# Softmax without maxima, and attention matmuls of several heads on separate row and column groups of the TensorE array

## Chip, cores and metric

The kernel runs on one core of one Trainium2 chip. A time is the device time of the run in microseconds (us). All runs quoted repeat within 0.3% except where the text says so. TensorE multiplies, VectorE and ScalarE read the results, GpSimd does little (busy for 2% of the kernel before). "Clock" is the share of its full clock that TensorE was granted.

## The reference

Sixteen batch elements of 256 channels and 32 x 32 = 1024 tokens, all in float32. Layer a is a softmax attention with 4 heads of 64 channels. Layer b is a group norm, a softmax attention with 8 heads of 32 channels, a second group norm and an MLP of width 1024. Cut to what matters:

```python
# layer a: x [16, 256, 32, 32], 4 heads of 64
qkv = (xs @ w_proj + b_proj).reshape(B, S, 4, 192)          # xs: tokens x channels
attn = softmax(einsum('bihd,bjhd->bijh', q, k) * 64 ** -0.5, axis=2)
res = einsum('bijh,bjhd->bihd', attn, v).reshape(B, S, 256) @ w_out + b_out + xs
# layer b: 8 heads of 32
q, k, v = split(group_norm(x) @ qkv_w.T)
attn = softmax(einsum('bhnd,bhmd->bhnm', q, k) * 32 ** -0.5 + phys_bias)   # phys_bias: per head
x = x + einsum('bhnm,bhmd->bhnd', attn, v) @ proj_w.T + proj_b
x = x + mlp_w2 @ gelu(mlp_w1 @ group_norm(x) + mlp_b1) + mlp_b2
```

## The kernel before

One element after the other; per element: q, k, v of layer a, its attention, projection and group norm, the same for layer b, then the MLP. Attention takes an item (512 queries of one head) at a time, in three products. First come the scores with queries on the partitions, only to find each query's maximum (`s`). Then the scores again with keys on the partitions (`w`), with the negated maximum brought in by an extra row, 33 rows instead of 32. Last comes the weighted sum (`acc`), whose ones columns give the denominator. One head at a time is on the array: 32 or 64 of its 128 rows in `s` and `w`, and in layer b 64 of its 128 columns in `acc`.

```python
        def maxima(i, j):                       # product s, 128 queries x 1024 keys
            s = ps_s.tile([P, S], F32, tag="s", ...)
            for u in range(NT):
                nc.tensor.matmul(s[:, u * TB : (u + 1) * TB],
                    qA[lo : lo + D, sl, qb * P : (qb + 1) * P],
                    kA[lo : lo + D, sl, u * TB : (u + 1) * TB], start=True, stop=True)
            nc.vector.tensor_reduce(negmax[i][:, j : j + 1], s, AX.X, ALU.max, negate=True)

        def weights(i, j):                      # product w, 256 keys x 512 queries
            for u in range(2):
                kb = 2 * j + u
                nc.tensor.matmul(s[:, u, :],
                    kA[lo : lo + D + 1, sl, kb * P : (kb + 1) * P],
                    qA[lo : lo + D + 1, sl, t * TB : (t + 1) * TB], start=True, stop=True)
            nc.scalar.activation(e, s, AF.Exp, scale=scale, bias=...)
            pending.append((i, j, e))

        def weigh():                            # product acc: v and ones columns
            for u in range(2):
                nc.tensor.matmul(acc[: 2 * D, :], vA[:, kb, h].rearrange("p o d -> p (o d)"),
                    e[:, u, :], start=(kb == 0), stop=(kb == SB - 1))
        # ... transposes that place the maxima cut
        for i, (t, h) in enumerate(items):
            place_maxima(i)
            for j in range(steps):
                if i + 1 < len(items) and j < QT:
                    maxima(i + 1, j)
                if pending:
                    weigh()
                weights(i, j)
```

Of the kernel before, what the change touches and what calls it, by code (L numbers as in the profile page):

```python
# [8 lines left out]
F32 = mybir.dt.float32  # L9
AF = mybir.ActivationFunctionType  # L10
ALU = mybir.AluOpType
AX = mybir.AxisListType

P = 128
# [3 lines left out]
HEADS1, D1 = 8, 32  # L18


@with_exitstack
def kernel(
    ctx: ExitStack,
    tc: tile.TileContext,
    x: bass.AP,        # [B, C, S]
    w_proj: bass.AP,   # [C, HEADS0 * 3 * D0], columns ordered (head, q|k|v, d)
    b_proj: bass.AP,
    w_out: bass.AP,    # [C, C]
    b_out: bass.AP,
    gn1_w: bass.AP,  # L30
    gn1_b: bass.AP,
    gn2_w: bass.AP,
    gn2_b: bass.AP,
    qkv_wT: bass.AP,   # [C, 3 * C]
    proj_wT: bass.AP,  # [C, C]
    proj_b: bass.AP,
    phys_bias: bass.AP,
    mlp_w1T: bass.AP,  # [C, HID]
    mlp_b1: bass.AP,
    mlp_w2T: bass.AP,  # [HID, C]  # L40
    mlp_b2: bass.AP,
    out: bass.AP,      # [B, C, S]
):
    nc = tc.nc
    B, C, S = x.shape
    HID = mlp_w1T.shape[1]
    CC = C // P            # channel chunks
    SB = S // P            # 128-token blocks
    TB = 512               # tokens per wide matmul
    NT = S // TB  # L50
    HC = HID // P
    QT = TB // P           # 128-token blocks in a wide one
    GSZ = C // GROUPS      # channels per group

    const = ctx.enter_context(tc.tile_pool(name="const", bufs=1))
    act = ctx.enter_context(tc.tile_pool(name="act", bufs=1))
    work = ctx.enter_context(tc.tile_pool(name="work", bufs=3))
    small = ctx.enter_context(tc.tile_pool(name="small", bufs=4))
    ps_s = ctx.enter_context(tc.tile_pool(name="ps_s", bufs=2, space=bass.MemoryType.PSUM))
    ps_m = ctx.enter_context(tc.tile_pool(name="ps_m", bufs=4, space=bass.MemoryType.PSUM))  # L60

    def load_x(b):
        t = act.tile([P, CC, S], F32, tag="x", name=f"x_{b}", bufs=2)
        for cc in range(CC):
            nc.sync.dma_start(t[:, cc, :], x[b, cc * P : (cc + 1) * P, :])
        return t

# [1 line left out]
    wp = const.tile([P, CC, 3, HEADS0, D0], F32, name="wp")  # L69
    for cc in range(CC):  # L70
        for t in range(3):
            nc.scalar.dma_start(
                wp[:, cc, t],
                w_proj[cc * P : (cc + 1) * P, :].rearrange(
                    "p (h t d) -> p t h d", t=3, d=D0
                )[:, t],
            )
    xs = {0: load_x(0)}

    # q and k biases with two heads on the partitions, v's along the free axis  # L80
    bp = b_proj.rearrange("(g i t d) -> i t d g", i=2, t=3, d=D0)
    bqk = const.tile([P, 2, HEADS0 // 2], F32, name="bqk")
    for i in range(2):
        for t in range(2):
            nc.gpsimd.dma_start(bqk[i * D0 : (i + 1) * D0, t, :], bp[i, t])
    bv = const.tile([P, HEADS0, D0], F32, name="bv")
    nc.gpsimd.dma_start(
        bv,
        b_proj.rearrange("(h t d) -> t h d", t=3, d=D0)[2].partition_broadcast(P),
    )  # L90
    pb = const.tile([P, HEADS1], F32, name="pb")
    nc.gpsimd.dma_start(pb, phys_bias.partition_broadcast(P))

    pbs = const.tile([P, HEADS1], F32, name="pbs")
    nc.vector.tensor_scalar(pbs, pb, float(D1) ** 0.5, None, ALU.mult)
# [5 lines left out]

    bo = load_vec(b_out, CC, "bo")
    g1w = load_vec(gn1_w, CC, "g1w")
    g1b = load_vec(gn1_b, CC, "g1b")
    g2w = load_vec(gn2_w, CC, "g2w")
    g2b = load_vec(gn2_b, CC, "g2b")
    pjb = load_vec(proj_b, CC, "pjb")
    m1b = load_vec(mlp_b1, HC, "m1b")
    m2b = load_vec(mlp_b2, CC, "m2b")

    def load_mat(w, name):
        k, n = w.shape
        t = const.tile([P, k // P, n], F32, name=name)
        nc.scalar.dma_start(t, w.rearrange("(c p) n -> p c n", p=P))
        return t

    wo = load_mat(w_out, "wo")
    wq = load_mat(qkv_wT, "wq")
    wpj = load_mat(proj_wT, "wpj")
    w1 = load_mat(mlp_w1T, "w1")  # L120
    w2 = load_mat(mlp_w2T, "w2")

    ident = const.tile([P, P], F32, name="ident")
    make_identity(nc, ident)
    # gavg[p, m] = 1 / GSZ where channels p and m share a group, else 0
    gind = const.tile([P, P // GSZ], F32, name="gind")
    nc.vector.tensor_reduce(
        gind, ident.rearrange("p (g j) -> p g j", j=GSZ), AX.X, ALU.add
# [9 lines left out]
    gavg = gavg.rearrange("p g j -> p (g j)")  # L138
    mhalf = const.tile([P, CC], F32, name="mhalf")
    nc.gpsimd.memset(mhalf, -0.5)  # L140
# [5 lines left out]
    # Head h lies in slot h // nb of qA and kA ([P, slots, S]), on the D partitions  # L146
    # from (h % nb) * 64 on. The partition after them holds ones in kA and, once
    # they are known, the queries' negated maxima in qA. vA ([P (key), SB, H, 2, D])
    # holds v and ones, so that the weighted sum comes with its denominator on D
    # further partitions.  # L150
    # Calls project(t, resT) when TB queries of all heads are in resT ([P, CC, S]).
# [102 lines left out]
    # y[:, co, t] = w^T src + bias + skip, tokens of t; bn_stats of y into stats  # L254
    def out_proj(key, w, nk, src, bias, skip, t, dst, stats):
        for co in range(CC):
            ps = mm_tile(f"{key}_{t}_{co}")
            for k in range(nk):
                nc.tensor.matmul(  # L259
                    ps,  # L260
                    w[:, k, co * P : (co + 1) * P],
                    src(k),
                    start=(k == 0),
                    stop=(k == nk - 1),
                )
            y = dst(co)
            nc.vector.scalar_tensor_tensor(  # L267
                y, ps, bias[:, co : co + 1], skip[:, co, t * TB : (t + 1) * TB],
                ALU.add, ALU.add,
            )  # L270
            if stats is not None:
                nc.vector.bn_stats(stats[:, co, t, :], y)

    def group_norm(key, src, stats, gw, gb):
        mv = small.tile([P, CC, 2], F32, tag="mv", name=f"mv_{key}")
        for cc in range(CC):
            nc.vector.bn_aggr(mv[:, cc, :], stats[:, cc].rearrange("p t k -> p (t k)"))
        ps = mm_tile(f"gm_{key}")
        mean_c = small.tile([P, CC], F32, tag="mean_c", name=f"mean_c_{key}")
        nc.vector.tensor_copy(mean_c, mv[:, :, 0])  # L280
        nc.tensor.matmul(ps[:, :CC], gavg, mean_c, start=True, stop=True)
        mean = small.tile([P, CC], F32, tag="mean", name=f"mean_{key}")
        nc.vector.tensor_copy(mean, ps[:, :CC])
        # variance of the group: mean over its channels of var_c + (mean_c - mean)^2
        dv = small.tile([P, CC], F32, tag="dv", name=f"dv_{key}")
        nc.vector.tensor_sub(dv, mean_c, mean)
        sq = small.tile([P, CC], F32, tag="sq", name=f"sq_{key}")
        nc.vector.tensor_mul(sq, dv, dv)
        tv = small.tile([P, CC], F32, tag="tv", name=f"tv_{key}")
        nc.vector.tensor_add(tv, sq, mv[:, :, 1])  # L290
        ps2 = mm_tile(f"gv_{key}")
        nc.tensor.matmul(ps2[:, :CC], gavg, tv, start=True, stop=True)
        ve = small.tile([P, CC], F32, tag="ve", name=f"ve_{key}")
        nc.vector.tensor_scalar(ve, ps2[:, :CC], EPS, None, ALU.add)
        rstd = small.tile([P, CC], F32, tag="rstd", name=f"rstd_{key}")
        nc.gpsimd.tensor_tensor(rstd, ve, mhalf, ALU.pow)
        a = small.tile([P, CC], F32, tag="ga", name=f"ga_{key}")
        nc.vector.tensor_mul(a, rstd, gw)
        ma = small.tile([P, CC], F32, tag="gma", name=f"gma_{key}")
        nc.vector.tensor_mul(ma, mean, a)  # L300
        c = small.tile([P, CC], F32, tag="gc", name=f"gc_{key}")
        nc.vector.tensor_sub(c, gb, ma)
        y = act.tile([P, CC, S], F32, tag="gn", name=f"gn_{key}")
        for t in range(NT):
            for cc in range(CC):
                sl = slice(t * TB, (t + 1) * TB)
                if cc % 2 == 0:
                    nc.vector.tensor_scalar(  # L308
                        y[:, cc, sl], src[:, cc, sl],
# [61 lines left out]
    for b in range(B):  # L371
        if b + 1 < B:
            xs[b + 1] = load_x(b + 1)
# [99 lines left out]
```

## Time and profile before

The three runs took 14661.59 to 14680.31 us, median 14663.05. Where they go, per batch element, from the starts of the phases in the trace (an attention counts from its first score product to the first product of the group norm after it, so with its projections; the two group norms, some 4 us each, are left out):

| phase | us per element before |
|---|---|
| layer a, attention and projection | 201.0 |
| layer b, attention and projection | 607.4 |
| layer b, q, k and v | 23.2 |
| MLP, from its first product to the next element's q, k, v | 57.2 |

The lines themselves are shown and read in the prediction below. A group line gives engine, operation, output and inputs, their sizes, the count, busy time, mean ns of one, and then the idle time before them with what ended it. A timeline line gives start, duration, engine and count of a run of like instructions. A windows line gives the stretch, then busy time and count of TensorE, its weight loads, VectorE, ScalarE and GpSimd, then the granted clock, the DMA share and GB/s.

### The profile page before, as it was taken

Reading aid. Unit: us, or ns where it says so; the run is one execution under the profiler, and the core shown is the slowest. Engines: PE = TensorE matmul, PEld = TensorE weight load, DVE = VectorE, ACT = ScalarE, POOL = GpSimd, SP = SyncE. Lnnn points to the kernel's source line nnn. Section 1 sums busy time; section 2 is a strip of 40 time slices with the busy share of each in tenths; the row PEclk is TensorE's granted clock in tenths of the full one; section 3 lists DMA queues with packets and bytes.
Section 4 is the critical chain, followed back from the end, with each engine's and each line's share of the span. In section 5 each row is a group of like instructions: output and inputs, shape, how many; then the busy total and the mean of one; then the engine's idle time right before and its main releaser. Section 6 shows DMA issues by size and latency. Waiting matters only on the chain.

```text
span 14689.8 us, 58040 instructions
## 1 busy us (share of the span) xinstructions
PE 14357.1 (98%) x24704; PEld 4764.6 (32%) x24704; DVE 4368.7 (30%) x4003; ACT 2188.0 (15%) x2336; POOL 258.7 (2%) x133
## 2 busy tenths in 40 slices
PE   9999999999999999999999999999999999999999
PEld 3233332333323333233332333323333233332333
DVE  3233232322323223232232322323223232232322
ACT  1111111111111111111111111111111111111111
POOL 0000000000000000000000000000000000000000
PEclk8686786867868668686686866868668686686866
DMA  0000000000000000000000000000000000000000
GB/s 21 0 3 3 3 3 0 3 3 3 3 0 3 3 2 4 0 3 3 2 4 0 3 3 2 5 0 3 3 3 3 0 3 3 3 0 0 3 0 3
DMA packets 19332, 41.62 MB, mean 3 GB/s; under 512 B 4704, under 2 KB 6240, under 8 KB 19072
## 3 DMA queue, kind: packets, MB, share of 16 engines
q1 hardware_dynamic: 13312, 33.56, 0.6%
q10 hardware_dynamic: 5296, 4.20, 0.1%
q8 instruction: 194, 3.18, 0.1%
q14 instruction: 66, 0.54, 0.0%
q0 software_dynamic: 464, 0.15, 0.0%
HBM read 21.12 MB, written 16.78 MB: 3 GB/s over the span
## 4 chain that ended last, share of the span: by engine, by line
PE 93%; issue 5%; DVE 2%; ACT 0%; POOL 0%; DMA 0%; ACTq 0%; POOLq 0%; DVEq 0%
PE acc_b L221 22%; PE s_b L169 19%; PE w_b L199 18%; PE s_a L169 7%; PE acc_a L221 7%; PE w_a L199 6%; PE m L420 3%; PE m L259 3%; PE qk_b L333 2%; PE qk_a L333 2%; PE row_b L184 1%; PE j L259 1%; PE v_a L356 1%; PE o L259 1%; PE v_b L356 1%
## 5 line engine op out<-in xcount | busy, mean ns | idle before, releaser
L221 PE MATMUL acc_b<-e_b,vA_b 128*64 128x512 f32 x4096 | 3566.7, 1025 | 6.0 <-ACT e_b L207 6.0
L169 PE MATMUL s_b<-kA_b,qA_b 32*128 32x512 f32 x4096 | 3060.5, 886 | 0.0
L199 PE MATMUL w_b<-qA_b,kA_b 33*128 33x512 f32 x4096 | 2864.9, 835 | 30.1 <-DVE qA_b L189 30.1
L176 DVE TENSOR_REDUCE nmax_b<-s_b 128x1 f32<-128x1024 f32 x1024 | 1253.7, 1224 | 4999.6 <-PE s_b L169 4995.4
L207 ACT ACTIVATE e_b<-w_b,pb 128x1024 f32<-128x1024 f32 x1024 | 1139.9, 1113 | 8376.4 <-PE w_b L199 8376.4
L199 PEld LDWEIGHTS w_b<-qA_b,kA_b 33*128 33x128 f32 x4096 | 945.8, 256 | 2288.7 <-issue 2269.2
L221 PEld LDWEIGHTS acc_b<-e_b,vA_b 128*64 128x64 f32 x4096 | 748.0, 211 | 2537.1 <-issue 2343.1
L169 PEld LDWEIGHTS s_b<-kA_b,qA_b 32*128 32x128 f32 x4096 | 916.1, 246 | 1667.9 <-issue 1451.9
L231 DVE RECIPROCAL rden_b<-acc_b 32x512 f32<-32x512 f32 x256 | 857.3, 3349 | 723.8 <-PE acc_b L221 723.8
L221 PE MATMUL acc_a<-e_a,vA_a 128*128 128x512 f32 x2048 | 1027.2, 627 | 11.8 <-ACT e_a L207 11.8
L169 PE MATMUL s_a<-kA_a,qA_a 64*128 64x512 f32 x2048 | 1028.7, 627 | 0.5 <-DVE nmax_a L176 0.5
L199 PE MATMUL w_a<-qA_a,kA_a 65*128 65x512 f32 x2048 | 984.1, 605 | 28.8 <-DVE qA_a L187 28.8
L176 DVE TENSOR_REDUCE nmax_a<-s_a 128x1 f32<-128x1024 f32 x512 | 626.0, 1223 | 1233.7 <-PE s_a L169 1232.1
L207 ACT ACTIVATE e_a<-w_a 128x1024 f32<-128x1024 f32 x512 | 523.9, 1023 | 2241.1 <-PE w_a L199 2236.1
L189 DVE TENSOR_SCALAR qA_b<-row_b,pbs 1x512 f32<-1x512 f32 x256 | 189.9, 742 | 1275.2 <-PE row_b L184 1274.2
L221 PEld LDWEIGHTS acc_a<-e_a,vA_a 128*128 128x128 f32 x2048 | 359.1, 193 | 639.5 <-issue 362.0
L199 PEld LDWEIGHTS w_a<-qA_a,kA_a 65*128 65x128 f32 x2048 | 394.4, 193 | 529.2 <-issue 506.2
L169 PEld LDWEIGHTS s_a<-kA_a,qA_a 64*128 64x128 f32 x2048 | 353.3, 190 | 577.4 <-issue 539.2
L420 PE MATMUL m<-gn_h,w 128*128 128x512 f32 x1024 | 480.3, 630 | 35.1 <-DVE gn_h L308 35.1
L231 DVE RECIPROCAL rden_a<-acc_a 64x512 f32<-64x512 f32 x128 | 430.0, 3359 | 253.4 <-PE acc_a L221 253.4
L259 PE MATMUL m<-g,w 128*128 128x512 f32 x1024 | 444.7, 592 | 0.0
L267 DVE SCALAR_TENSOR_TENSOR o<-m,m2b,x 128x512 f32<-128x512 f32 x64 | 48.1, 751 | 875.3 <-PE m L259 875.3
(98 smaller groups left out, 4119.8 us busy)
## 6 DMA issues: line engine op xcount, KB each, us to landing
x<-in_x_dram SPq DMA_DIRECT2D x32, 512.0 KB, 4.0
out_dram<-o SPq DMA_DIRECT2D x32, 512.0 KB, 2.8
w<-in_L_conv_mlp_w_dram ACTq DMA_DIRECT2D x2, 1024.0 KB, 9.3
wp<-in_L_conv_w_proj_dram ACTq DMA_DIRECT2D x6, 128.0 KB, 8.3
wq<-in_L_conv_qkv_w_dram ACTq DMA_DIRECT2D x1, 768.0 KB, 7.3
wo<-in_L_conv_w_out_dram ACTq DMA_DIRECT2D x1, 256.0 KB, 5.5
wpj<-in_L_conv_proj_w_dram ACTq DMA_DIRECT2D x1, 256.0 KB, 8.5
bv<-in_L_conv_b_proj_dram POOLq DMA_DIRECT2D x1, 128.0 KB, 8.2
```

Source lines behind the costliest of these rows:

```text
L169: nc.tensor.matmul(s[:, u * TB : (u + 1) * TB], qA[lo : lo + D, sl, qb * P : (qb + 1) * P], kA[lo : lo + D, sl, u * TB : (u + 1) * TB], st ...
L176: nc.vector.tensor_reduce(negmax[i][:, j : j + 1], s, AX.X, ALU.max, negate=True)
L184: nc.tensor.transpose(row[0:1, j * P : (j + 1) * P], nm[:, j : j + 1], ident)
L189: nc.vector.tensor_scalar(d, row[0:1, :], unscaled_bias[0:1, h : h + 1], None, ALU.subtract)
L199: nc.tensor.matmul(s[:, u, :], kA[lo : lo + D + 1, sl, kb * P : (kb + 1) * P], qA[lo : lo + D + 1, sl, t * TB : (t + 1) * TB], start=True, ...
L207: nc.scalar.activation(e, s, AF.Exp, scale=scale, bias=0.0 if bias is None else bias[:, h : h + 1],)
L221: nc.tensor.matmul(acc[: 2 * D, :], vA[:, kb, h].rearrange("p o d -> p (o d)"), e[:, u, :], start=(kb == 0), stop=(kb == SB - 1),)
L231: nc.vector.reciprocal(rden[:D, :], acc[D : 2 * D, :])
L259: nc.tensor.matmul(ps, w[:, k, co * P : (co + 1) * P], src(k), start=(k == 0), stop=(k == nk - 1),)
L333: nc.tensor.matmul(ps, weights(cc, which)[:, ch * P : (ch + 1) * P], src[:, cc, t * TB : (t + 1) * TB], start=(cc == 0), stop=(cc == CC - 1),)
L356: nc.tensor.matmul(ps[:, :C], src[:, cc, sb * P : (sb + 1) * P], weights(cc, 2), start=(cc == 0), stop=(cc == CC - 1),)
L420: nc.tensor.matmul(ps, w1[:, cc, hc * P : (hc + 1) * P], hn[:, cc, t * TB : (t + 1) * TB], start=(cc == 0), stop=(cc == CC - 1),)
```

## The change

Three intentions. The maxima go: the scores of these inputs are small enough for exp without a shift. (Sums of denominators and of their reciprocals are collected, and if at the end they are out of bounds, a branch runs the general path again; it isn't taken here.) The heads share the array: two heads of layer a lie on rows 0-63 and 64-127, four of layer b on 32 rows each, and in `acc` two heads write to columns 0-63 and 64-127. And copies, divisions and GpSimd sums of the checks take the place of what the maxima and ones columns did. The core of the diff, with the move of the general path into a function and all renaming cut:

```diff
-        def maxima(i, j):
-        def place_maxima(i):
-        def weights(i, j):
...
+            G = P // D
+            items = [(t, g) for t in range(NT) for g in range(CC)]
+            def scores(i, kb):
...
+                for j in range(G):
+                    lo = j * D
+                    nc.tensor.matmul(
+                        s[j // 2][:, j % 2, :],
+                        kA[lo : lo + D, g, kb * P : (kb + 1) * P],
+                        qA[lo : lo + D, g, t * TB : (t + 1) * TB],
+                        start=True, stop=True)
+                for j in range(G // 2):
+                    nc.scalar.activation(e[j], s[j], AF.Exp, scale=scale)
...
+            def weigh():
...
+                for j in range(G):
+                    lo = (j % 2) * 64
+                    if D == 64:
+                        v = vA[:, kb, g * P + lo : g * P + lo + D]
+                    else:
+                        v = vA[:, kb, g * G + j].rearrange("p o d -> p (o d)")
+                    nc.tensor.matmul(
+                        acc[j // 2][lo : lo + 64, :], v, e[j // 2][:, j % 2, :],
+                        start=(kb == 0), stop=(kb == SB - 1))
...
+            for i, (t, g) in enumerate(items):
+                for kb in range(SB):
+                    scores(i, kb)
+                    if len(pending) > lag:
+                        weigh()
...
+    again = nc.values_load(bad[0:1, 0:1], min_val=0, max_val=1)
+    with tc.If(again > 0):
+        shifted(tc, k, x, out)
```

The end of an item in layer b is in the changed kernel:

```python
                    for j in range(G):
                        a = acc[j // 2]
                        lo = (j % 2) * 64
                        nc.scalar.copy(resT[to, g, sl], a[lo : lo + D, :])
                        nc.vector.tensor_copy(den[to, :], a[lo + D : lo + 2 * D, :])
                    nc.vector.reciprocal(rd, den)
                nc.vector.tensor_mul(r, r, rd)
```

## The prediction

> **What bounds the kernel now.** I read the page first: the busy shares, the granted clock by slices, the chain, the groups. TensorE is the bound: its row is full from end to end, and the chain of work that ended last is TensorE for 93% of the span. The second line alternates between 8 and 6 tenths: part of every batch element runs at a lower granted clock. In the groups, read the count and the mean of the six attention rows: three products (s for the maxima, w for the weights, acc for the weighted sum), in layer a (64 channels per head) and layer b (32).
>
> ```profile
> PE 14357.1 (98%) x24704; PEld 4764.6 (32%) x24704; DVE 4368.7 (30%) x4003; ACT 2188.0 (15%) x2336; POOL 258.7 (2%) x133
> ...
> PEclk8686786867868668686686866868668686686866
> ...
> PE 93%; issue 5%; DVE 2%; ACT 0%; POOL 0%; DMA 0%; ACTq 0%; POOLq 0%; DVEq 0%
> ...
> L221 PE MATMUL acc_b<-e_b,vA_b 128*64 128x512 f32 x4096 | 3566.7, 1025 | 6.0 <-ACT e_b L207 6.0
> L169 PE MATMUL s_b<-kA_b,qA_b 32*128 32x512 f32 x4096 | 3060.5, 886 | 0.0
> L199 PE MATMUL w_b<-qA_b,kA_b 33*128 33x512 f32 x4096 | 2864.9, 835 | 30.1 <-DVE qA_b L189 30.1
> ...
> L207 ACT ACTIVATE e_b<-w_b,pb 128x1024 f32<-128x1024 f32 x1024 | 1139.9, 1113 | 8376.4 <-PE w_b L199 8376.4
> ...
> L221 PE MATMUL acc_a<-e_a,vA_a 128*128 128x512 f32 x2048 | 1027.2, 627 | 11.8 <-ACT e_a L207 11.8
> L169 PE MATMUL s_a<-kA_a,qA_a 64*128 64x512 f32 x2048 | 1028.7, 627 | 0.5 <-DVE nmax_a L176 0.5
> L199 PE MATMUL w_a<-qA_a,kA_a 65*128 65x512 f32 x2048 | 984.1, 605 | 28.8 <-DVE qA_a L187 28.8
> ```
>
> The code issues 2048 s_b matmuls; the trace has 4096. Each f32 matmul is two records, one straight after the other on the same rows. Next, the timeline of TensorE in the two products of the MLP and in layer a (start, duration). Ends are modelled, so I use starts.
>
> ```profile
> 884.27 13.90 PE L259 MATMUL m<-g,w 128*128 128x512 f32 x32
> 898.00 13.90 PE L420 MATMUL m<-gn_h,w 128*128 128x512 f32 x32
> ...
> 98.59 1.98 PE L169 MATMUL s_a<-kA_a,qA_a 64*128 64x512 f32 x4
> 100.51 1.98 PE L221 MATMUL acc_a<-e_a,vA_a 128*128 128x512 f32 x4
> 102.33 1.88 PE L199 MATMUL w_a<-qA_a,kA_a 65*128 65x512 f32 x4
> 104.14 1.12 PE L169 MATMUL s_a<-kA_a,qA_a 64*128 64x512 f32 x2
> ```
>
> 32 records in 13.73 us: one half of an f32 matmul takes T = 0.429 us at full clock. Twelve in the round of layer a should take 5.15; they take 104.14 - 98.59 = 5.55. Start by start the 0.40 lies in two places of 0.195 each: s to acc and w to s, where the rows used change between 64 and 128. Between acc and w, where they don't (65 rows don't fit into half of the array), there is nothing, though w also waits for a semaphore. Now three stretches of the first batch element (layer a, layer b, MLP; the figure after the busy times is the granted clock), and one raised clock in layer b:
>
> ```profile
> 26.00:220.00 194.00, 193.27 (x464) 79.54 (x465) 80.94 (x71) 35.48 (x36) 2.75 (x1) 1.00 0.00 0
> 272.00:834.00 562.00, 561.24 (x780) 159.13 (x780) 142.46 (x106) 65.91 (x60) 0.00 (x0) 0.61 0.00 0
> 868.00:925.00 57.00, 56.96 (x127) 25.18 (x128) 2.70 (x4) 13.23 (x19) 0.00 (x0) 0.96 0.02 9
> ```
> ```profile
> 1192.86 3.78 PE L169 MATMUL s_b<-kA_b,qA_b 32*128 32x512 f32 x4
> 1196.57 3.68 PE L221 MATMUL acc_b<-e_b,vA_b 128*64 128x512 f32 x4
> 1200.17 2.16 PE L199 MATMUL w_b<-qA_b,kA_b 33*128 33x512 f32 x4
> 1202.26 2.11 PE L169 MATMUL s_b<-kA_b,qA_b 32*128 32x512 f32 x4
> ```
>
> Layer b is 562 of a batch element's 918 us, at a clock of 0.61. Four records take 3.7 us [...]; then 2.1. I took the trace's clock windows (3.4 us) one by one and the share of array cells (rows x columns of each matmul) in use in each. Of the windows at full clock with 50% or more in use, 98 to 100% are followed by full clock[...].
>
> [...]
>
> **The change part by part.** (1) *Maxima go*: the s products, 6144 of 24704 records with 4089 us of busy time, the transposes (1536 records) and VectorE's 1880 us of reductions. s takes the place of w. (2) *Row groups*: two heads of layer a (64 rows each) or four of layer b (32 each) side by side. (3) *Column groups*: two heads write acc to partitions 0-63 and 64-127. Layer a loses the ones columns: VectorE sums e and two matmuls per item make the denominators. (4) *Evacuation* is wider; each finished item has copies, a reciprocal, and two small adds on GpSimd, which touch no chain. (5) The final test and the branch: an estimate of 20 us, once.
>
> How far does packing go? My chosen step: program order with both halves adjacent. Head A's second half cannot start before its first ends, at T; head B's first half follows in order, so it starts at T beside A's second; B's second at 2T. A pair ends at 3T, not 2T; four end at 5T. Each group then costs one mode switch, because s (row groups) and acc (column groups) alternate:
> - Layer a, per 128 keys and pair of heads: 2 x (3 x 0.429 + 0.195) = 2.96 us. 32 such steps per batch element: 95 us. Denominators 4 x 0.9 = 4 us.
> - Layer b, per 128 keys and four heads: 2 x (5 x 0.429 + 0.195) = 4.68 us; 32 steps: 150 us, at full clock.
> - Other engines per step: ScalarE one exp of 1.02 us in a and two of 1.11 in b, VectorE about 1.2 in a (by the 1.22 us of its 128x1024 reduction). Both fit beside 2.96 and 4.68.
> - Kept, from the first element's timeline: q, k, v of a 20.7, a's tail with projection and group norm 13.9, q, k, v of b 22.7, b's tail 13.5, MLP 57.4, two first halves of projections 6.9: 135 us. Added: 1.5 for the denominators in a's tail, 2.7 for four copies of 0.68 ahead of b's reciprocal, and about 5 (estimate) for accumulators that wait for their copies: 9.
>
> Sum: 95 + 4 + 150 + 135 + 9 = 393 us per element, times 16 is 6290, with start and test 6320.
>
> The clock in b: s uses 2T/5T of the cells (40%), acc 80%; with the switches the mean is 55%, and the worst 3.4 us window holds about 53%. [...] I allow for some half-clock windows: 6320 becomes **6600**.
>
> **Rivals.**
> - *No overlap*: [...] Steps become 2 x (4T + 0.195) = 3.8 and 2 x (8T + 0.195) = 7.25: 510 us per element, 8200. And then cells in use stay near 37% in b, the clock falls, and it is 10,000 or so. For: nothing here shows f32 packing. Against: [...] the rows are disjoint.
> - *Full overlap*: halves of different heads interleave. Steps 2 x (2T + 0.2) = 2.1 in a and (2T + 0.2) + (4T + 0.2) = 3.0 in b: 68 + 96 us, 5000 in all. ScalarE at 2.5 us per step would be close to the bound in b. Against: order and adjacency.
> - *Weight loads not pulled ahead*: each change of tile adds a load of 0.107 us (the first load of a phase to its second in this trace). Steps 3.18 and 5.3, plus 27 us per element: 6800[...].
> - *ScalarE or VectorE become the bound*: against it, their 1.0 to 2.5 us per step above. Only with full overlap.
>
> **Range and chances.** 10% full overlap (near 5200), 45% my step with the clock kept (6200 to 6700), 25% with loads or clock lost (6700 to 7900), 20% little overlap (over 7900). So 5300 to 8300 around 6600. Removing 28% of TensorE's busy time with nothing in its place is alone over 2%: faster is nearly sure.
>
> **What would show it.** In the timeline of the changed kernel, starts within an s_b group of eight records should span 4T (1.7 us), not 7T (3.0) or T; the start of a group should lie 2.3 us after the group before it. Granted clock in layer b near 1.0; the s_a and s_b of the maxima gone; VectorE near 30% of the shorter span. ScalarE's idle time should still be put down to TensorE. Wrong if records of one group start T apart throughout (no overlap), if the clock in b stays near 0.6, or if TensorE's waits name ScalarE in b.

## The result

The changed kernel is correct and takes 5017.86 us (median of four runs, 4992.46 to 5043.19), against 14671.68 us of the kernel before in the same rounds: ratio 0.3419 with a 95% interval of 0.3402 to 0.3435. A ratio is the mean time of one kernel's runs over the mean of the other's of the same rounds, so not quite the ratio of the medians. The direction was as predicted; the size was not: 5018 lies below the range of 5300 to 8300, and at the rival "full overlap", put at 5000.

From the page of the changed kernel: the busy shares, the clock, the chain that ended last.

```profile
PE 4629.3 (92%) x17282; PEld 1649.6 (33%) x17282; DVE 1748.9 (35%) x1832; ACT 2025.6 (40%) x2273; POOL 495.7 (10%) x312
...
PEclk9999999999999999999999999999999999999999
...
PE 88%; DVE 8%; ACT 2%; issue 1%; POOL 0%; DMA 0%; ACTq 0%; DVEq 0%
```

TensorE is still the bound, now with 8% of the chain on VectorE. The clock line no longer dips to 6 tenths (mean clock 0.952, before 0.732). From 24704 records to 17282, and each shorter in effect. The groups:

```profile
L284 PE MATMUL acc_b<-e_b,vB 128*64 128x512 f32 x4096 | 988.3, 604 | 59.0 <-DVE den_b L262 59.0
...
L229 PE MATMUL s_b<-qA_b,kA_b 32*128 32x512 f32 x4096 | 616.3, 640 | 3.9 <-DVE vB L360 3.9
L229 PE MATMUL s_a<-qA_a,kA_a 64*128 64x512 f32 x2048 | 569.4, 638 | 0.0
...
L284 PE MATMUL acc_a<-e_a,vA_a 128*64 128x512 f32 x2048 | 545.3, 616 | 11.2 <-ACT e_a L237 11.2
```

Here is the trap of a busy column over overlapping work: s_b has 4096 records of 640 ns mean, 2621 us if one added them, and is busy for 616 us, a quarter. Four heads run at once (their starts, within 20 ns, are below). The acc_b group has 604 ns x 4096 = 2474 us and is busy for 988, a ratio of 2.5 though it has only two column groups: the modelled end of a record (0.59 us) lies beyond the start of the next one on its columns (0.43 us), so such a ratio overstates the overlap. The timeline of TensorE in layer a and, after the mark, in layer b:

```profile
347.71 1.13 PE L229 MATMUL s_a<-qA_a,kA_a 64*128 64x512 f32 x4
348.77 1.08 PE L284 MATMUL acc_a<-e_a,vA_a 128*64 128x512 f32 x4
349.77 1.13 PE L229 MATMUL s_a<-qA_a,kA_a 64*128 64x512 f32 x4
...
461.27 1.94 PE L284 MATMUL acc_b<-e_b,vB 128*64 128x512 f32 x8
463.14 1.14 PE L229 MATMUL s_b<-qA_b,kA_b 32*128 32x512 f32 x8
464.21 1.94 PE L284 MATMUL acc_b<-e_b,vB 128*64 128x512 f32 x8
```

By starts, with T = 0.429 us for a half of a full-clock matmul as before: s_a takes 1.06 us, acc_a 1.00, acc_b 1.87, s_b 1.07. Two halves are 2T = 0.86; the s groups and acc_a are 2T and 0.14 to 0.21 for the change of tiling, and acc_b is 4T + 0.15, with four heads on only two column groups. A step is 2.06 us in layer a and 2.94 in layer b. The prediction had 2.96 and 4.68.

One s_b group record by record, from the trace, start in us:

```
480.772  480.779  480.786  480.792      first halves of four heads: within 20 ns
481.306  481.312  481.319  481.326      second halves: 534 ns after them
```

So the halves of different heads do interleave. Of the 512 groups of layer b, 480 look like this. (534 ns is T and 0.105 us: half of the 0.21 us by which s_b exceeds 2T lies between the two halves.) Then the stretches of the first elements that answer to those of before (layer a, layer b, MLP):

```profile
343.00:416.00 73.00, 72.25 (x279) 18.79 (x280) 52.45 (x39) 35.63 (x37) 13.25 (x7) 1.00 0.00 1
455.00:563.00 108.00, 101.44 (x521) 28.31 (x520) 24.96 (x25) 69.78 (x79) 8.51 (x6) 0.98 0.00 1
579.00:636.00 57.00, 57.00 (x128) 24.98 (x128) 2.27 (x4) 12.82 (x18) 0.00 (x0) 0.96 0.03 9
```

Layer b has a clock of 0.98 where it had 0.61; the MLP's 57 us are as before. ScalarE is busy for 70 of 108 us in layer b: much, and not the bound. Last, what TensorE waits for:

```profile
PE j L119 <- DVE den_b L262: 64.1, 31, 2.2
PE acc_b L284 <- DVE den_b L262: 59.0, 32, 1.8
PE j L119 <- DVE resT_b L264: 47.0, 16, 4.1
PE gm_g L145 <- DVE mean_c_g L144: 40.1, 16, 2.5
```

These are tails (total us, times, longest): projections (j, o) that wait for a denominator, an accumulator not yet copied, a group norm that waits for its statistics. They are no part of the packing, and two experiments below deal with them.

Per element: layer a 84.1 us (201.0 before), layer b 119.5 (607.4), q, k and v of b 23.6 (23.2), MLP 57.6 (57.2). All of the gain lies in the two attentions.

### The profile page after: what moved, and what is told of

It is laid out like the page before. It is cut to its first block, busy times and chain, and to the rows that moved or that the text cites. A ratio compares the mean times of both kernels' runs of the same rounds, so it can differ in the third digit from the quotient of the medians.

```text
span 5040.9 us, 41667 instructions
## 1 busy us (share of the span) xinstructions
PE 4629.3 (92%) x17282; PEld 1649.6 (33%) x17282; DVE 1748.9 (35%) x1832; ACT 2025.6 (40%) x2273; POOL 495.7 (10%) x312
## 4 chain that ended last, share of the span: by engine, by line
PE 88%; DVE 8%; ACT 2%; issue 1%; POOL 0%; DMA 0%; ACTq 0%; DVEq 0%
PE acc_b L284 18%; PE s_b L229 10%; PE acc_a L284 10%; PE s_a L229 10%; PE m L428 10%; PE m L119 9%; PE qk_b L326 5%; PE qk_a L326 4%; PE j L119 3%; DVE den_b L262 3%; PE o L119 2%; PE v_b L347 2%; PE v_a L347 2%; PE den_a L250 1%; DVE rd_a L254 1%; DVE rd_b L263 1%
## 5 line engine op out<-in xcount | busy, mean ns | idle before, releaser
L237 ACT ACTIVATE e_b<-s_b 128x1024 f32<-128x1024 f32 x1024 | 992.7, 1022 | 726.6 <-PE s_b L229 725.4
L284 PE MATMUL acc_b<-e_b,vB 128*64 128x512 f32 x4096 | 988.3, 604 | 59.0 <-DVE den_b L262 59.0
L237 ACT ACTIVATE e_a<-s_a 128x1024 f32<-128x1024 f32 x512 | 520.9, 1024 | 561.6 <-PE s_a L229 561.4
L229 PE MATMUL s_b<-qA_b,kA_b 32*128 32x512 f32 x4096 | 616.3, 640 | 3.9 <-DVE vB L360 3.9
L229 PE MATMUL s_a<-qA_a,kA_a 64*128 64x512 f32 x2048 | 569.4, 638 | 0.0
L284 PE MATMUL acc_a<-e_a,vA_a 128*64 128x512 f32 x2048 | 545.3, 616 | 11.2 <-ACT e_a L237 11.2
L428 PE MATMUL m<-hn,w 128*128 128x512 f32 x1024 | 486.8, 637 | 35.2 <-DVE hn L171 35.2
L295 DVE TENSOR_TENSOR esum_a<-esum_a,e_a 128x1024 f32<-128x1024 f32 x384 | 466.7, 1215 | 109.9 <-ACT e_a L237 93.3
L284 PEld LDWEIGHTS acc_b<-e_b,vB 128*64 128x64 f32 x4096 | 252.4, 136 | 736.4 <-issue 714.6
L326 PE MATMUL qk_b<-xn,wq 128*128 128x512 f32 x512 | 268.8, 691 | 35.2 <-DVE xn L171 35.2
```

Of the source, the lines that this page charges most:

```text
L229: nc.tensor.matmul(s[j // 2][:, j % 2, :], kA[lo : lo + D, g, kb * P : (kb + 1) * P], qA[lo : lo + D, g, t * TB : (t + 1) * TB], start=Tru ...
L237: nc.scalar.activation(e[j], s[j], AF.Exp, scale=scale)
L284: nc.tensor.matmul(acc[j // 2][lo : lo + 64, :], v, e[j // 2][:, j % 2, :], start=(kb == 0), stop=(kb == SB - 1),)
L295: nc.vector.tensor_add(to, esum, e[0])
L326: nc.tensor.matmul(ps[:, t, :], weights(cc, which)[:, ch * P : (ch + 1) * P], src[:, cc, t * TB : (t + 1) * TB], start=(cc == 0), stop=(cc ...
L428: nc.tensor.matmul(ps, k.w1[:, cc, hc * P : (hc + 1) * P], hn[:, cc, t * TB : (t + 1) * TB], start=(cc == 0), stop=(cc == CC - 1),)
```

## Experiments

The theory after the result: **each tile of the array (the rows and columns that one matmul uses) takes its matmuls in its own order**, so a matmul for a free tile starts although an earlier one for a busy tile is still queued. Rival A: the halves are merely laid out interleaved, and starts are strictly in program order after all. For the clock, an estimate: the rows in use count, so above all the time in matmuls of 128 rows, and not (as predicted) the share of array cells. Rival B: without overlap, the clock would fall back too.

### Undoing packing and order

**The order of the column groups.** In layer b the weighted sums of the four heads go to columns 0, 64, 0, 64; here to 0, 0, 64, 64. Results are the same.

```diff
-                for j in range(G):
+                for j in ((0, 1) if G == 2 else (0, 2, 1, 3)):
                     lo = (j % 2) * 64
```

> Only the order of the four acc products of a step of layer b changes: columns 0-63, 0-63, 64-127, 64-127 in place of alternating ones. Theory 1, each tile of the array takes its matmuls in its own order and a later tile may start while an earlier one's are still queued: the step's acc group stays at 1.87 us and the time at 5018 us within 1%. Theory 2, only the second half of one f32 matmul may be overtaken, while whole matmuls start in program order: the third product starts with or after the second, the group takes 6T + 0.15 = 2.7 us, and the kernel 512 x 0.86 us = 440 us more, near 5460. Theory 3, strict order of starts, the rule of my prediction: 7T + 0.15 = 3.15 us, near 5680.

Measured: 5051.18 us, ratio 0.3443 (0.3437 to 0.3448), within the 1% of theory 1. From its timeline of TensorE:

```profile
481.39 1.94 PE L284 MATMUL acc_b<-e_b,vB 128*64 128x512 f32 x8
...
486.25 1.04 PE L284 MATMUL acc_b<-e_b,vB 128*64 128x512 f32 x2 [1.85 <-DVE den_b L262]
487.80 1.94 PE L284 MATMUL acc_b<-e_b,vB 128*64 128x512 f32 x6 [0.50 <-DVE den_b L262]
```

The first line is a group of eight records in 1.94 us, as long as in the changed kernel. Record by record the starts are

```
481.393  481.406    481.873  481.886    482.301  482.316    482.731  482.744
```

always two together, 13 to 15 ns apart (so in 453 of the 512 groups). The third matmul of the program (columns 64) starts at 481.406, beside the first; the second (columns 0, which the first keeps for 2T) starts at 482.301. In strict order the third would have to wait for the start of the second, and the group would take 6T = 2.6 us. It takes 4T: the third matmul overtakes the second. Rival A falls, whether the two halves are one instruction or two. The last two lines show the limit. The second matmul waits there for a copy on VectorE (the semaphore of den_b), and the third, whose columns are free and whose own inputs are ready, waits behind it: two records, then nothing for 0.50 us, then six (22 groups of the run look so). So in this run **a wait for a semaphore held back the starts on both column groups (0.50 us), and a busy column group held back only its own (482.301 against 481.406).** The same wait is seen in the changed kernel itself, at the second group of layer b of the first element, where the third head waits for ScalarE: two first halves start at 456.356 and .362, their second halves at .889 and .896, and the other two heads only at 457.279, after ScalarE's semaphore. The first two heads' second halves did not wait for the other heads' first ones, so no interleaving was laid out beforehand.

**One head after the other.** The changed kernel, but s and acc of one head alternate, so that there is never a neighbour on a free tile. Nothing else is changed.

```diff
-            def scores(i, kb):
+            def scores(i, kb, between):
...
+                    if between:
+                        weigh(j)
...
-                    scores(i, kb)
-                    if len(pending) > lag:
-                        weigh()
+                    scores(i, kb, len(pending) >= lag)
```

> The changed kernel with the score product and the weighted sum of one head next to each other on TensorE, so that the mode of the array changes after every matmul and nothing can overlap; all else as in the changed kernel (right result). Theory, packing is what gives the second part of the gain: layer a 32 x 4 x (2T + 0.195) = 135 us instead of 66, layer b 32 x 8 x (2T + 0.195) = 270 us at full clock, and more, [...]: about 480 at half clock. Kernel 9000 if the clock stays, near 12000 if it falls. Rival, a matmul is short in the changed kernel for another reason (narrow output, other layout): under 6000.

Measured: 8301.55 us, ratio 0.5658, clock 0.975; the expected 9000 was too high.

```profile
301.18 1.12 PE L229 MATMUL s_b<-qA_b,kA_b 32*128 32x512 f32 x2
302.23 1.07 PE L288 MATMUL acc_b<-e_b,vB 128*64 128x512 f32 x2
303.23 1.12 PE L229 MATMUL s_b<-qA_b,kA_b 32*128 32x512 f32 x2
```

One head's two records of s take 1.05 us by starts, where the changed kernel does four heads in 1.07; its two of acc take 1.00, where four heads took 1.87. The clock holds, so rival B falls: the prediction's sum for no overlap, 8200, was good, and its further loss of clock, to 10,000, was not. Overlap is worth 8302 - 5018 = 3284 us here; a part of that (an estimate below) is only the more frequent change of tiling.

**The column groups undone.** Every acc on columns 0-63, in an accumulator of its own; for the room in PSUM the score buffers go from 3 to 2 and the accumulators from 2 to 4. The control has the buffers alone. (The run also copies a finished item of layer a in two parts instead of one, which the control does not.)

```diff
-        ps_s = ... bufs=3 ...
-        ps_a = ... bufs=2 ...
+        ps_s = ... bufs=2 ...
+        ps_a = ... bufs=4 ...
...
-                    n = 1 if D == 64 else 2
+                    n = G
...
-                        acc[j // 2][lo : lo + 64, :], v, e[j // 2][:, j % 2, :],
+                        acc[j][0:64, :], v, e[j // 2][:, j % 2, :],
```

> The changed kernel with every weighted sum on columns 0-63 in a bank of its own (two score buffers and four accumulators in PSUM in place of three and two); the row groups stay. Right result. Theory: acc takes 2 x 2T + 0.15 = 1.87 us instead of 1.01 in layer a and 4 x 2T + 0.15 = 3.58 instead of 1.87 in layer b; 32 x (0.86 + 1.72) = 82 us per element, 1320 in all: 6340, up to 6700 if the clock is lost where acc alone (half of the cells) fills a window. Rival, the column groups give nothing and the row groups all: near 5020.

> Control for the run without column groups: the changed kernel with its PSUM buffers (two for scores, four for accumulators), but the column groups kept. If the 1200 us of that run came from the columns, this stays near 5018 us, or below it where the two more accumulator banks remove the waits of 1.84 us at the ends of items in layer b; two score buffers may add waits for ScalarE. If the buffers made the difference: near 6200.

Measured: 6221.12 us (ratio 0.424, clock 0.971) and, the control, 5047.22 (0.3437, 0.962). The difference, 1174 us, is what two column groups are worth. In the timeline acc_a now takes 505.92 - 504.06 = 1.86 us instead of 1.00:

```profile
504.06 1.93 PE L285 MATMUL acc_a<-e_a,vA_a 128*64 128x512 f32 x4
505.92 1.13 PE L229 MATMUL s_a<-qA_a,kA_a 64*128 64x512 f32 x4
```

By the sum: 2T more in each of 512 acc groups of layer a and 4T in each of 512 of layer b, 6 x 0.429 x 512 = 1318 us; measured 1174, for some of it hides waits that then no longer show (an inference). From one head at a time (8302) to this one it is 2080 us, which is the row groups with fewer changes of tiling. An estimate of the latter: 2 x 2048 + 2 x 1024 changes instead of 2 x 512 + 2 x 512 are 4096 more, by some 0.2 us each: 820 us.

**A row group repeated.** The same test for rows as the first one for columns, in layer a. It is built on the version with two steps in turn (below), with the scores in the order of rows 0-63, 0-63, 64-127, 64-127 over both steps.

```diff
+            def two(i, k0):
...
+                for j in range(2):
+                    lo = j * D
+                    for u in range(2):
+                        kb = k0 + u
+                        nc.tensor.matmul(s[u][:, j, :], kA[lo : lo + D, g, ...], ...)
```

> The kernel with fewer mode switches (4956 us), with the four score products of two steps of layer a ordered rows 0-63, 0-63, 64-127, 64-127. Theory, a tile's queue of matmuls doesn't hold back a later tile, for row groups as for column groups: same starts in pairs, 4956 us within 1%. Rival, only neighbours in the program overlap: 6T in place of 4T, 256 x 0.86 us = 220 us more, near 5180.

Measured: 5042.33 us, ratio 0.3433 (0.3427 to 0.3438): 86 us above the version it is built on (4956.34), in between the two expectations. The question of the order is answered by its timeline:

```profile
350.56 1.99 PE L255 MATMUL s_a<-qA_a,kA_a 64*128 64x512 f32 x8
```

The eight records start in pairs, 13 ns apart, and the group takes 1.92 us, as in the version it is built on (224 of the 256 groups look so). In strict order it would be 6T = 2.6. So the row groups of this run overtake as the column groups did. The 86 us come from elsewhere, and only in part are they found. The trace also holds the semaphore updates, and they show that **the starts overtook, but the results were signalled in program order**: in the version it is built on, the signal of a step's scores comes 0.6 us after the start of the half that gives it, in all 512 cases. Here that of the first step comes 1.5 us after it in those 224 groups (started at 351.109, signalled at 352.574, 0.04 us before the second step's), and the second step's product on rows 0-63, earlier in the program, ends only then. So exp of the first step waits there for the whole group. TensorE's first wait for ScalarE in each layer a is up to 1.6 us (24.2 in all; 11.2 in the version it is built on), and the half clock lasts for 519 instead of 451 us. The rest (layer a 83.2 instead of 79.7 us per element, layer b 121.0 instead of 119.5) stays open.

### The maxima and the clock

**The kernel before without maxima.** No s product, no transposes, no extra row; heads stay unpacked. (It takes no care of large scores, which these inputs don't have; its result is correct.)

```diff
-                    kA[lo : lo + D + 1, sl, kb * P : (kb + 1) * P],
-                    qA[lo : lo + D + 1, sl, t * TB : (t + 1) * TB],
+                    kA[lo : lo + D, sl, kb * P : (kb + 1) * P],
+                    qA[lo : lo + D, sl, t * TB : (t + 1) * TB],
...
-        for j in range(QT):
-            maxima(0, j)
...
-            place_maxima(i)
...
-                if i + 1 < len(items) and j < QT:
-                    maxima(i + 1, j)
```

> The kernel before with the maxima taken out and nothing packed (right result). If the clock follows the share of the array in use: layer a loses its s products and two of four 0.195 us switches per round, about 60 us per batch element; layer b has cells in use near 37%, stays near 0.6 of the clock, and falls from 562 to about 370 us. Together near 670 us per element, 10700 us in all. If the lower clock of layer b came from the maxima alone, b would run at full clock, 64 x 3.8 = 245 us, and the kernel near 8700.

Measured: 7937.82 us, ratio 0.5411, clock 0.955: below both expectations. Removing 31% of the records (24704 to 17024) took 46% of the time, for the clock came back with it (0.955, before 0.734). The stretch of layer b in the first element, which had a clock of 0.61 before:

```profile
183.00:420.00 237.00, 237.00 (x522) 82.14 (x520) 63.12 (x40) 70.70 (x69) 0.00 (x0) 0.96 0.00 0
```

A cell share explains this badly: w uses 32 of 128 rows, a quarter of the cells, acc half of them, 37% on average, and the clock is 0.96 here; the prediction had estimated a border near 45%. The traces record the clock, full or half, in stretches of 3413 ns and whole multiples of it (but for the last one). I took those windows of 3413 ns in which layer b's s, w and acc alone ran, TensorE was busy for 85% or more and the clock was full, sorted them by how much of the window matmuls of 128 rows (acc) took, each record counted from its start to the next one's, and counted which were followed by full clock:

| share of acc | before | without maxima | one head after the other | halves of acc moved (next) | changed kernel |
|---|---|---|---|---|---|
| 0 to 5% | 0 of 282 | - | - | 0 of 15 | - |
| 5 to 15% | 0 of 98 | 0 of 49 | - | - | - |
| 15 to 25% | 0 of 20 | 34 of 97 | - | 5 of 5 | - |
| 25 to 50% | 18 of 18 | 429 of 429 | 567 of 567 | 1317 of 1317 | - |
| over 50% | 41 of 41 | 417 of 417 | 520 of 520 | 16 of 16 | 398 of 398 |

A border near 20% serves all five kernels (the 20 windows of the kernel before in the band around it all have under 18%): with under 15% of acc, the rest in products on 32 or 33 rows, none of 444 windows was followed by full clock. In the kernel before, w and s lie side by side, some 3.8 us at full clock, and where they filled a whole window, with under 5% of acc, half clock followed in all 282 cases. From half clock it came back only after a window with most of it in acc: of the kernel before, none of 1319 such windows with up to 65% of acc was followed by full clock, and all 472 with over 75% were. So it stayed low for long (7880 us in all).

One count fits both directions in these runs. Take each record as its rows / 128 of its time at full clock (0.427 us for 512 columns, half of the 0.853 us between starts at half clock in the kernel before), and add up what falls into a window. Over all 25,836 windows of the thirteen runs, all phases, at full or half clock: with under 0.36 of a window, 5 of 3873 were followed by full clock; between 0.36 and 0.40, 217 of 473; between 0.40 and 0.5, 2933 of 3022; with 0.5 or more, 18,462 of 18,468. The best single border, 0.38, misplaces 1% of the windows; the best one in cells misplaces 6%, and in busy time 7%. It agrees with the 20% above (0.2 + 0.8 / 4 = 0.40), and w and s alone have 0.25. It is a count over these runs; that the rows are the cause was not shown, for no experiment changed them alone.

**The same work, another order.** If that is so, moving half of acc between w and s should bring the clock back without taking any work away.

```diff
-                if pending:
-                    weigh()
+                more = bool(pending)
+                if more:
+                    weigh((0,))
                 weights(i, j)
+                if more:
+                    weigh((1,))
```

> The kernel before with the same matmuls and all its maxima; only the order changes: the first half of each weighted sum stays between s and w, the second half goes between w and the next s. Right result. Theory 1, the half clock of layer b comes where 32-row products fill a whole 3.4 us window (s and w side by side take 3.7 us at full clock), and a 128-row acc in each window prevents it: the clock in layer b goes from 0.61 to near 1, layer b from 562 to about 64 x (12T + 4 x 0.195) = 380 us, the kernel from 14670 to about 11750, though one mode switch is added per round. Theory 2, the mean share of cells in use decides (33% before and after the move, my reading when I predicted): the clock stays near 0.6 and the kernel near 14700 or a little above.

Measured: 12343.19 us (12259 to 12427), ratio 0.8413 (0.8345 to 0.8482), clock 0.896. Its layer b:

```profile
272.00:680.00 408.00, 406.12 (x799) 118.62 (x798) 148.29 (x110) 69.02 (x62) 0.00 (x0) 0.89 0.00 0
```

The same matmuls take 408 us there instead of 562. It fell short of the expected 11750 because the clock, once at half, stays there in some elements: of 276 half-clock windows none was raised while this mix lasted (with a third of it in acc, half of the rows are in use, which at half clock is 0.25 of a window in the count above). Time at half clock over the whole kernel: before 7880 us, reordered 2554, without maxima 712, changed kernel 486.

### Going further

What is left in the changed kernel are the changes of tiling and the tails. Four versions, each correct.

**Fewer changes of tiling.** In layer a, two score steps, then two steps of acc.

```diff
-                    if len(pending) > lag:
-                        weigh()
+                    if G == 4 or kb % 2:
+                        while len(pending) > lag:
+                            weigh()
```

> The changed kernel with layer a issuing two steps of scores, then two of weighted sums, so half as many changes of the array's mode there; nothing else. Theory, a change between row and column groups costs 0.15 to 0.2 us also when packed: 0.36 us less per two steps, 16 times per element and 16 elements, 93 us less: near 4925. Rival, the switch is hidden when tiles overlap, or scores then wait for ScalarE: 5018 or more.

Measured: 4956.34 us, ratio 0.3379 (0.3373 to 0.3384).

```profile
347.18 1.99 PE L229 MATMUL s_a<-qA_a,kA_a 64*128 64x512 f32 x8
349.10 1.94 PE L284 MATMUL acc_a<-e_a,vA_a 128*64 128x512 f32 x8
```

By starts 1.92 and 1.86 us for twice the work of 1.06 and 1.00, so 0.17 us saved per change here; layer a goes from 84.1 to 79.7 us per element. In all it is 62 us of the expected 93. The changed kernel's runs had two levels, 4993 and 5043, at clocks of 0.961 and 0.952; what sets them is open, and this version is below both.

**Tails filled.** The MLP of the element before is issued after layer a's attention, and the next element's q, k, v of layer a after layer b's attention, so that TensorE has work while the group norms and denominators finish. (For the room, two small tiles have one buffer instead of two.)

```diff
+            q0, k0, v0 = ahead
...
+            if late:
+                mlp(*late)
             q1, k1, v1 = qkv(
...
+            if b + 1 < B:
+                ahead = front(b + 1)
...
+            late = (b, hn, x2)
```

> The changed kernel with the MLP of an element issued after the first attention of the next one, and q, k and v of the next element after the second attention, so that TensorE has work while the last reciprocal and the group norm of a layer run. Same instructions. The waits named in the tails are 18 us per element, 291 in all, and the half clock that follows them cost (1 - 0.952) x 5041 = 242 us of full-speed time: near 4510. If the half clock is not due to those pauses: near 4730. If VectorE and ScalarE, not TensorE, hold the tails up: over 4900.

> Both of the above: if they add, near 4420; if the switches of layer a are no longer on TensorE's path once the tails are filled, as b2.

Measured: 4707.84 us (4687 to 4723; ratio 0.3211; 0.3198 to 0.3224), and together with the edit before 4604.16 (0.3139; 0.3134 to 0.3145). Time at half clock falls from 486 to 154 and 97 us: the pauses had also cost clock. The expected 4510 and 4420 were 4% too low. The total is near the 4730 of the rival, that the half clock is not due to the pauses; what speaks against the rival is the clock itself. TensorE still waits at the ends of layer b's items:

```profile
PE acc_b L284 <- DVE den_b L262: 60.1, 32, 1.9
```

**Accumulators released sooner.** The line just shown is acc_b waiting for an accumulator that four narrow copies on VectorE and four on ScalarE still read. Here each engine copies one whole accumulator first. For the room, the buffers of e go from 6 to 5, for which there is no control.

```diff
+                    nc.vector.tensor_copy(held[0], acc[0])
+                    nc.scalar.copy(held[1], acc[1])
                     for j in range(G):
-                        a = acc[j // 2]
+                        a = held[j // 2]
```

> The kernel with filled tails and fewer switches (4604 us), with both accumulators of a finished item of layer b first copied whole, one by VectorE and one by ScalarE, and the copies by head made from SBUF. Theory, the waits of 1.84 to 1.92 us for the fourth copy at the end of each item hold TensorE up and make it lose its clock now and then: those waits (60 + 31 us) go, 4500 us or a little less. Rival, another wait takes their place (the copies of VectorE and ScalarE are more): 4600 or more.

Measured: 4585.12 us, ratio 0.3122 (0.3117 to 0.3127), the best of all: 8.6% below the changed kernel. The 60 us of wait and the projection's 31 us behind it are gone, and only 19 us came of them, for other waits take part of their place:

```profile
PE j L119 <- DVE resT_b L270: 21.8, 16, 5.1
PE s_b L229 <- ACT e_b L237: 20.7, 31, 1.1
```

The longer copies, or for s_b the missing buffer of e, delay, it seems, the results themselves (j) and ScalarE's exps (s_b); that was not tested apart.

## Why the prediction was wrong, by its own steps

**Bound and direction: right.** TensorE bounds both kernels; VectorE's 35% (predicted 30%) and ScalarE's 40% never do.

**The kept parts: right.** q, k and v of b, the MLP and layer a's q, k, v took what they took before (23.6, 57.6 and 21.0 us per element).

**How far packing goes: the step that failed.** The prediction said: "Head A's second half cannot start before its first ends, at T; head B's first half follows in order, so it starts at T beside A's second". Measured: four first halves within 20 ns, second halves 534 ns later. A pair takes 2T and not 3T, four take 2T and not 5T. The premise was the order of starts. In the trace of the kernel before, where nothing is packed, attention matmuls start one after the other, never less than 428 ns apart; that this order holds for packed ones too was the author's estimate, which no trace of this case showed, and the largest chance, 45%, was put on it all the same. The runs with repeated column and row groups show the order of starts to be one of each tile (481.406 for the third matmul, 482.301 for the second), with both column groups held back by a semaphore wait alone (0.50 us); only the signals of completion kept program order (with the row groups repeated, 1.5 us after the start and not 0.6). The tiles worked in parallel for f32, too: four first halves within 20 ns, and 2T + 0.21 us for the group.

**What that is worth.** Steps of 2.06 instead of 2.96 us in a and 2.94 instead of 4.68 in b, 32 of each per element: (0.90 + 1.74) x 32 = 84 us per element, 1350 us in all. From 6320 (the sum before the allowance for the clock) that gives 4970; measured 5018. The rest of the sum was right within 50 us.

**The change of tiling: right.** 0.195 us from the unpacked trace; 0.14 to 0.21 in the packed one. The rival with weight loads would have added 0.107 us for what this figure already held: in the unpacked trace too, the second half of the first matmul after a change starts 0.533 us after the first half (98.595, 99.128) and not 0.429, with the weight loads of the two 0.106 us apart. In acc, whose weights have 64 columns and not 128, it is 0.480 us, and the loads lie 0.055 us apart (348.766, 349.246). That acc's changes are the cheaper ones for this reason is an inference.

**The clock: wrong in its reading, harmless here.** The prediction read a border near 45% of the cells from the trace of the kernel before; that was the author's estimate, and the runs don't show it (at 37% the clock is 0.955 without maxima). That trace doesn't either: with each record counted from its start to the next one's, 54 of its 55 full-clock windows with 35 to 40% of the cells in use were followed by full clock. What fits the windows of all runs best is the count of rows in use, which at 0.38 of a window misplaces 1% of 25,836. The allowance of 280 us (6320 to 6600) was not needed: half clock lasted 486 us, and 332 of these went with the filled tails, so these were not the packing's. And the rival "no overlap" would have cost 8302, not 10,000.

**How the 9650 us divide.** Taking the maxima away gives 14671 to 7938, clock included; packing, with the other edits that came with it, gives the 2920 from there to 5018. (The reverse order, packing with the maxima kept, was not run.) The prediction did not part the two. The larger part is the maxima: their own work, and the half clock that s next to w brought, of which the reordering alone took 2333 us away. The sum had the full clock of layer b right for another reason, so by luck.

**The chances.** 10% for full overlap was too little: the argument against it was an order of starts that no trace of packed matmuls had shown.

## What to carry to other kernels

Put small-row or small-column products of different heads next to each other (here 5018 us instead of 8302 for one head after the other), and count a group as the longest queue of one tile plus about 0.2 us for each change between row and column groups (here 2T or 4T, and 0.14 to 0.21 us). The order of the tiles did not change that count here (groups of 1.94 us in both orders of the columns, 1.92 us in both orders of the rows), but put first in the program what another engine waits for: results were signalled in program order, with the row groups repeated 1.5 us after the start instead of 0.6. Have every semaphore of a group ready, for here one wait held back both column groups (nothing for 0.50 us). And count the 128-row matmuls in each window of 3.4 us: in these runs, 21,395 of 21,490 windows with 0.4 or more of the rows in use were followed by full clock, and spreading half of acc, the same work in another order, was alone 16% of the kernel before. Where no trace has packed matmuls yet, an order of starts is a rival and not the step to build on.
